# A deformable convolution and an embedding moved into the slots of an attention layer

## The chip, the cores and the metric

One core of a Trainium2 chip runs one program. It has five engines with a queue of instructions each: TensorE (PE), VectorE (DVE), ScalarE (ACT), GpSimd (POOL) and SyncE (SP), which issues most DMAs. An engine works through its queue in order and waits on semaphores for the others. The metric is device microseconds of one execution. The kernel before takes 12436.45 us, the median of 3 runs (12427.92 to 12447.01).

## The reference

Four layers follow each other on four images of 128 channels and 48x48 = 2304 positions: a selective scan (layer 0), a deformable convolution (layer 1), linear attention (layer 2), softmax attention (layer 3); after each of the last two comes a mixture of experts. What the change touches is layer 1 and the beginning of layer 2. Layer 1 samples the image at 9 taps per position, each at coordinates shifted by a small convolution's output, interpolates between four corners, and multiplies by a weight per tap:

```python
y0f = jnp.floor(py)
x0f = jnp.floor(px)
...
return v00 * (1 - wy) * (1 - wx) + v01 * (1 - wy) * wx + v10 * wy * (1 - wx) + v11 * wy * wx
...
sampled = _bilinear_gather(x, py, px) * mask[:, None]
out = jnp.einsum('oik,bikhw->bohw', weight.reshape(Co, C, 9), sampled)
...
return jax.nn.relu(out)
```

Layer 2 first normalises each position over its channels and embeds it, `h = x @ tok_W + tok_b + pe[None]`. Then follow eight blocks of attention over a whole image (each with its own weights), in which a position's keys are summed over the image before any query uses them, and a feed-forward part:

```python
t = t + attn(layer_norm(t, ln1_g[i], ln1_b[i]), i)
u = layer_norm(t, ln2_g[i], ln2_b[i])
t = t + (jax.nn.gelu(u @ W1[i] + b1[i], approximate=False) @ W2[i] + b2[i])
```

## The kernel before

Positions lie on the 128 partitions, channels in the free dimension. A tile is 128 positions (18 an image, `NT`), a block 3 tiles (384 positions; 6 an image, `NBLK`, 24 in all, `NBL`). The state `T`, called `h` in layer 2, holds all 72 tiles in SBUF.

Layer 0 writes each image to a table in DRAM, in which a row holds the four corners of one position (4 x 128 numbers), and the 27 offsets of each position to `offs`.

Layer 1 is `_layer1`. For each image, DVE makes from the offsets the table row of each tap (`idx`) and four corner weights with the mask in them (`wq`), in lines 949 to 982. Then tile after tile: POOL issues one gather of 128 table rows per tap into `g` (line 990; eight buffers), DVE multiplies the four corners by their weights into `gw` (line 997; four buffers), and PE multiplies each corner by the identity, which turns positions to the free dimension and adds the four up in PSUM (line 1003). ScalarE copies three taps at a time to `sT` (line 1006), PE multiplies nine taps by their weights (line 1009), adds the bias (line 1010), and ScalarE applies Relu (line 1011). The order of this part is left to a scheduler.

`_layer2` then embeds: for each image it measures means and deviations (`measure`, `finish`: batch statistics on DVE, a power on POOL), normalises (`normed`, line 1134), transposes (`transposed`, line 1146), multiplies by `tok_w` (line 1167) and adds `pe`, in which POOL has added the token's bias to the positions (line 1151). It keeps a copy of the layer's input in DRAM (`kept`) for the residual at the end.

The eight attention layers run as one chain of slots, whose order is written out by hand for PE, ACT, DVE and POOL. In slot s, counted through the layers at 24 blocks each, the key steps k1, k2, k3 work on block s; the query steps q0 to q2 on block s - 9 (`LAG`), q3 to q6 on block s - 10; the feed-forward f0 on block s - 11, f1 and f2 on s - 12 (`FLAG`), f3 and f4 on s - 13. So slots 0 to 8 hold key steps only, from 9 on queries join, from 12 on everything is there. After each image's sixth key block, `pieces` (the exponentials of the keys and the products `context`) are spread over the next slots. k0 normalises the next block on POOL and f0 on DVE; `biased` adds an output bias to a block of the state on POOL, right behind each of these two norms; `rotated` ends with an addition on POOL. The next layer's weights are created at slot 16 of a layer and prepared at slot 21.

A block of the code that sets the pace of layer 1:

```python
nc.gpsimd.indirect_dma_start(
...
gw = sp.tile([P, 4, C], F32, name="gw", bufs=4)
nc.vector.tensor_mul(
...
for q in range(4):
    nc.tensor.matmul(
        pt[:, t - t0, :], gw[:, q, :], ident, start=q == 0, stop=q == 3
    )
```

Of the kernel before, what the change touches and what calls it, by code (L numbers as in the profile page):

```python
# [15 lines left out]
F32 = mybir.dt.float32  # L16
# [894 lines left out]

def layer1(env, io, table, offs, T):


    with ExitStack() as ctx:
        _layer1(ctx, env, io, table, offs, T)


def _layer1(ctx, env, io, table, offs, T):
    nc, tc, ident = env.nc, env.tc, env.ident  # L920
    cp = ctx.enter_context(tc.tile_pool(name="l1c", bufs=1))
    sp = ctx.enter_context(tc.tile_pool(name="l1s", bufs=2))
    ps = ctx.enter_context(tc.tile_pool(name="l1p", bufs=3, space=PSUM))
    po = ctx.enter_context(tc.tile_pool(name="l1o", bufs=2, space=PSUM))
# [3 lines left out]
    w = cp.tile([P, TAPS, C], F32, name="w")  # L928
    nc.sync.dma_start(w, io["l1_w"])


    def row(name):
        t = cp.tile([P, C], F32, name=name)
        nc.scalar.dma_start(t, io[name].to_broadcast([P, C]))
        return t

    scale, shift, mean, var = (row("l1_" + n) for n in ("gamma", "beta", "mean", "var"))
    nc.vector.tensor_scalar_add(var, var, 1e-5)
    nc.scalar.sqrt(var, var)
    nc.vector.reciprocal(var, var)  # L940
    nc.vector.tensor_mul(scale, scale, var)
    nc.vector.tensor_mul(mean, mean, scale)
    nc.vector.tensor_sub(shift, shift, mean)
    for t in range(TAPS):
        nc.vector.tensor_mul(w[:, t, :], w[:, t, :], scale)

    for b in range(NB):
# [35 lines left out]
        for i in range(NT):  # L983
            sT = sp.tile([P, TAPS, P], F32, name="sT")
            for t0 in range(0, TAPS, 3):
                pt = ps.tile([P, 3, P], F32, name="pt")
                for t in range(t0, t0 + 3):
                    g = sp.tile([P, 4 * C], F32, name="g", bufs=8)
                    j = i * TAPS + t
                    nc.gpsimd.indirect_dma_start(  # L990
                        out=g,
                        out_offset=None,
                        in_=table,
                        in_offset=bass.IndirectOffsetOnAxis(ap=idx[:, j : j + 1], axis=0),
                    )
                    gw = sp.tile([P, 4, C], F32, name="gw", bufs=4)
                    nc.vector.tensor_mul(  # L997
                        gw,
                        g.rearrange("p (q c) -> p q c", c=C),
                        wq[:, i, t, :].unsqueeze(2).to_broadcast([P, 4, C]),  # L1000
                    )
                    for q in range(4):
                        nc.tensor.matmul(  # L1003
                            pt[:, t - t0, :], gw[:, q, :], ident, start=q == 0, stop=q == 3
                        )
                nc.scalar.copy(sT[:, t0 : t0 + 3, :], pt)
            out = po.tile([P, C], F32, name="out")
            for t in range(TAPS):
                nc.tensor.matmul(out, sT[:, t, :], w[:, t, :], start=t == 0, stop=False)
            nc.tensor.matmul(out, env.ones_row, shift[:1, :], start=False, stop=True)  # L1010
            nc.scalar.activation(T[:, b * NT + i, :], out, AF.Relu)
# [25 lines left out]
def layer2(env, io, T):  # L1037


    with ExitStack() as ctx:  # L1040
        _layer2(ctx, env, io, T)
# [5 lines left out]
FLAG = LAG + 3  # L1047

# [6 lines left out]
def _layer2(ctx, env, io, T):  # L1055
# [33 lines left out]
    tok_b = cp.tile([P, 1, C], F32, name="tok_b")  # L1089
# [25 lines left out]
    def measure(st, b, j):  # L1115
        mv, rstd = st
        s6 = sp.tile([P, G3, nc.vector.BN_STATS_DIM], F32, name="s6", bufs=3)
        for g in range(G3):
            nc.vector.bn_stats(out=s6[:, g, :], in_=h[:, b * NT + j * G3 + g, :])
            nc.vector.bn_aggr(out=mv[:, j * G3 + g, :], in_=s6[:, g, :])  # L1120
# [8 lines left out]
    def normed(st, b, j, engine, name):  # L1129
        mv, rstd = st  # L1130
        xn = sp.tile([P, G3, C], F32, name=name, bufs=1)
        for g in range(G3):
            i = j * G3 + g
            engine.tensor_scalar(  # L1134
                xn[:, g, :],
                h[:, b * NT + i, :],
                mv[:, i, 0:1],
                rstd[:, i : i + 1],
                op0=ALU.subtract,
                op1=ALU.mult,  # L1140
            )
        return xn
# [5 lines left out]

    pe = bp.tile([P, NT, C], F32, name="dk")
    nc.scalar.dma_start(pe, io["l2_pe"])  # L1150
    nc.gpsimd.tensor_add(pe, pe, tok_b.to_broadcast([P, NT, C]))
    st1 = []
    for b in range(NB):
        first = stats()
        for j in range(NBLK):
            nc.sync.dma_start(kept[:, at(b, j), :], h[:, at(b, j), :])
            measure(first, b, j)
        finish(first, 0, NT)
        st1.append(stats())
        for j in range(NBLK):  # L1160
            pt = psum(P, BLK)
            transposed(normed(first, b, j, nc.vector, "fn"), pt)
            xT = sp.tile([P, BLK], F32, name="uT", bufs=1)
            nc.scalar.copy(xT, pt)
            pp = psum(P, G3, C)
            for g in range(G3):
                nc.tensor.matmul(pp[:, g, :], xT[:, bass.ts(g, P)], tok_w, start=True, stop=True)
            nc.vector.tensor_add(h[:, at(b, j), :], pp, pe[:, j * G3 : (j + 1) * G3, :])
            measure(st1[b], b, j)
        finish(st1[b], 0, NT)  # L1170
# [32 lines left out]

    def biased(w, r, b, j):
        hb = h[:, at(b, j), :]
        nc.gpsimd.tensor_add(hb, hb, w["bias"][:, r : r + 1, :].to_broadcast([P, G3, C]))  # L1206

    def rotated(w, name, b0, b1, xT, j):
# [12 lines left out]
        nc.gpsimd.tensor_add(q, q, r)  # L1221
# [20 lines left out]
    def k0(y, n):  # L1242
        t, s, b, j = block(y, n)
        t["xn"] = normed(y.first[b], b, j, nc.gpsimd, "kn")
        biased(y.w, 0, b, j)

    def k1(y, n):
        t, s, b, j = block(y, n)
        col = y.w["col"]
        if j % (NBLK // 2) == 0:  # L1250
# [7 lines left out]
        t["xT"] = sp.tile([P, BLK], F32, name="xT", bufs=LAG + 2)  # L1258
# [45 lines left out]
    def largest_keys(s):  # L1304
# [7 lines left out]
        def tokens():  # L1312
# [4 lines left out]
            s["xb"] = sp.tile([P, P], F32, name="xb")  # L1317
# [225 lines left out]
    with tc.manual_schedule(engines=ORDERED):  # L1543
        for slot in range(-1, NL * NBL + FLAG + 3):
            i, n = divmod(slot, NBL)
            if i + 1 < NL and n == FLAG + 4:
                layers[i + 1] = Layer(i + 1, layers[i].after)
            if i + 1 < NL and n == NBL - 3:
                prepare(layers[i + 1].w)
            do(q0, slot - LAG)  # L1550
            do(f1, slot - FLAG)
            do(m0, slot - FLAG - 2)
            do(k1, slot)
            some(1)
            do(q3, slot - LAG - 1)
            do(f3, slot - FLAG - 1)
            do(k2, slot)
            do(f2, slot - FLAG)
            do(m1, slot - FLAG - 2)
            some(1)  # L1560
            do(q1, slot - LAG)
            do(k0, slot + 1)
            do(q4, slot - LAG - 1)
            some(1)
            do(k3, slot)
            do(whole, slot)
            do(f0, slot - FLAG + 1)
            do(q5, slot - LAG - 1)
            some(1)
            do(q2, slot - LAG)  # L1570
            some(1)
            do(m2, slot - FLAG - 2)
            do(q6, slot - LAG - 1)
            do(f4, slot - FLAG - 1)
            do(m3, slot - FLAG - 2)

# [662 lines left out]
def program(tc, io, out):  # L2239
    with ExitStack() as ctx:  # L2240
        env = Env(ctx, tc)
        nc = tc.nc
        with ExitStack() as conv:
            dr = conv.enter_context(tc.tile_pool(name="dr", bufs=1, space=DRAM))
# [147 lines left out]
```

## Time and profile before

| | us |
|---|---|
| median of 3 runs | 12436.45 |
| the profiled execution | 12545.34 |
| its span, first to last instruction | 12543.6 |
| layer 0, and layer 1's preparation | 0 to 5255.8 |
| gathers and products of layer 1 | 5255.8 to 6276 |
| embedding | 6276 to 6403 |
| layer 2's slots 0 to 20 | 6403 to 6733.8 |
| its slots 21 to 191 begin | 6733.8 to 10442.9 |
| rest (end of layer 2, experts, layer 3, experts) | to 12543.6 |

Times inside the span are counted from its first instruction. PE was granted 0.949 of its clock on the mean. Over the span PE is busy 87%, DVE 68%, ACT 55%, POOL 35%. A line of the profile names the line of the program, the engine, the operation, the tile written and, behind the arrow, the tiles read; for a group it then gives the number of instructions, the time in which at least one was running, the mean duration of one in ns, and the idle time of the engine just before them with what ended it. PE's products of full 32-bit numbers appear as two records each.

### The profile page before, as it was taken

To read this page: it belongs to the slowest core of one execution; us is meant where nothing else is said; L and a number is where in the kernel's file an instruction comes from. 1 tells how busy PE (TensorE), PEld (TensorE's weight loads), DVE (VectorE), ACT (ScalarE), POOL (GpSimd) and SP (SyncE) were. 2 spreads that over 40 slices of the span, in tenths; PEclk is the share of its full clock that TensorE was granted. 3 is DMA by queue.
4 is the path that set the end of the run, shared out by engine and by line. 5 is a ranking of instruction groups with operands and counts; after the bars stand their busy time and mean duration, and the time that the engine had idled before them with its cause. 6 is when DMAs were issued, how large, how long until landed. Compare 5 with 4: busy or idle time off the path is not lost.

```text
span 12543.6 us, 192625 instructions
## 1 busy us (share of the span) xinstructions
PE 10872.6 (87%) x71008; PEld 8365.3 (67%) x71008; DVE 8487.3 (68%) x15484; ACT 6888.6 (55%) x13190; POOL 4409.7 (35%) x4799
## 2 busy tenths in 40 slices
PE   7788787978887787688879999999999999698897
PEld 6667666766676666588857777777777777333333
DVE  6998989888988899544456656566566565455554
ACT  5777767777777777411135655555556555232332
POOL 2433434333333343366633333333333332100001
PEclk9999999999999999899979999999999999799998
DMA  3221222122212222356500000000000000300003
GB/s 122 68 70 63 80 77 71 63 76 80 70 64 76 79 67 67 111 171 177 170 21 2 4 3 3 4 2 4 2 3 5 1 1 12 115 7 8 8 8 126
DMA packets 329879, 677.51 MB, mean 54 GB/s; under 512 B 41556, under 2 KB 152168, under 8 KB 328048
## 3 DMA queue, kind: packets, MB, share of 16 engines
q1 hardware_dynamic: 276064, 493.50, 12.3%
q0 software_dynamic: 51840, 169.91, 4.8%
q8 instruction: 570, 9.34, 0.3%
q14 instruction: 365, 2.99, 0.1%
q10 hardware_dynamic: 1040, 1.77, 0.0%
HBM read 602.63 MB, written 71.85 MB: 54 GB/s over the span
## 4 chain that ended last, share of the span: by engine, by line
PE 43%; DVE 7%; ACT 3%; issue 1%; DMA 1%; POOL 1%; another core or an unknown queue 0%; SPq 0%; ACTq 0%; DVEq 0%; POOLq 0%
PE psum L1466 4%; PE pt L1003 4%; PE psum L1458 4%; PE pc L1352 3%; PE psum L1402 3%; PE scT L2105 3%; PE sc L2052 3%; PE out L2134 3%; PE psum L1372 2%; PE psum L1212 2%; PE psum L1213 2%; PE psum L1146 2%; PE psum L1290 1%; PE psum L1391 1%; DVE mx L1375 1%
## 5 line engine op out<-in xcount | busy, mean ns | idle before, releaser
L576 ACT ACTIVATE hs<-ps,bct 128x256 f32<-128x256 f32 x4608 | 1853.8, 474 | 1174.9 <-PE ps L570 1122.5
L570 PE MATMUL ps<-ident,h 128*128 128x128 f32 x9216 | 1491.9, 294 | 783.4 <-DVE h L556 612.7
L570 PEld LDWEIGHTS ps<-ident,h 128*128 128x128 f32 x9216 | 1079.7, 148 | 1168.7 <-DVE h L556 720.3
L584 PE MATMUL yp<-ident,hs 128*128 128x128 f32 x9216 | 1399.3, 288 | 28.5 <-ACT ys L599 28.5
L516 ACT ACTIVATE dA<-delta,l_Al 128x768 f32<-128x768 f32 x1536 | 1388.2, 936 | 0.3
L523 POOL TENSOR_TENSOR h<-du,rB 128x512 f32<-128x512 f32 x768 | 1077.5, 1403 | 757.9 <-PE ps L570 683.1
L584 PEld LDWEIGHTS yp<-ident,hs 128*128 128x128 f32 x9216 | 1151.2, 150 | 83.6 <-ACT ys L599 57.6
L556 DVE TENSOR_TENSOR_SCAN h<-dA,h 128x256 f32<-128x256 f32 (+1 forms) x1024 | 1084.4, 1059 | 27.3
L556 DVE TENSOR_TENSOR_SCAN h<-dA,carry,h 128x768 f32<-128x768 f32 x512 | 1027.1, 2006 | 10.5 <-ACT dA L516 10.5
L1206 POOL TENSOR_TENSOR T<-T,bias 128x384 f32<-128x384 f32 x384 | 383.7, 999 | 1563.5 <-DVE fn L1134 1523.2
L498 POOL TENSOR_SCALAR_AFFINE_SELECT dB<-bct 128x512 f32<-128x512 f32 x768 | 746.0, 971 | 358.4 <-PE b L530 240.9
L2113 ACT ACTIVATE pT<-scT 128x768 f32<-128x768 f32 (+2 forms) x504 | 377.6, 749 | 841.0 <-PE scT L2105 838.9
L530 PE MATMUL b<-dB,duT 128*128 128x128 f32 x6144 | 828.3, 279 | 0.8 <-ACT duT L456 0.8
L556 DVE TENSOR_TENSOR_SCAN h<-dA,carry,b 128x512 f32<-128x512 f32 x512 | 645.7, 1261 | 263.1 <-PE b L530 242.7
L1003 PE MATMUL pt<-ident,gw 128*128 128x128 f32 x5184 | 685.1, 294 | 147.2 <-DVE gw L997 117.6
L990 POOL DMA_INDIRECT g<-table,idx x648 | 659.9, 1018 | 390.0 <-DVE gw L997 189.6
L530 PEld LDWEIGHTS b<-dB,duT 128*128 128x128 f32 x6144 | 768.6, 196 | 2.4 <-POOL h L523 1.2
L1003 PEld LDWEIGHTS pt<-ident,gw 128*128 128x128 f32 x5184 | 650.1, 207 | 176.9 <-DVE gw L997 110.6
L997 DVE TENSOR_TENSOR gw<-g,wq 128x512 f32<-128x512 f32 x648 | 428.7, 692 | 496.9 <-PE pt L1003 416.7
L563 POOL COPY carry<-h 128x2 f32<-128x2 f32 x512 | 96.8, 189 | 1782.0 <-DVE h L556 1717.7
L2062 DVE TENSOR_REDUCE mx<-sc 128x2 f32<-128x1024 f32 (+3 forms) x400 | 428.3, 1071 | 345.2 <-PE sc L2052 340.2
L527 DVE TENSOR_TENSOR h<-du,rB 128x512 f32<-128x512 f32 x768 | 638.7, 832 | 1.6 <-DMA rB<-rows 1.4
(394 smaller groups left out, 22833.0 us busy)
## 6 DMA issues: line engine op xcount, KB each, us to landing
rB<-rows SPq DMA_DIRECT2D x768, 384.0 KB
w<-f_w SPq DMA_DIRECT2D x64, 1024.0 KB
table<-zero SPq DMA_DIRECT2D x162, 128.0 KB
table<-tok SPq DMA_DIRECT2D x16, 1152.0 KB
g<-table,idx POOLq DMA_INDIRECT x648
yd<-y SPq DMA_DIRECT2D x4, 2304.0 KB
sums<-raw SPq DMA_DIRECT2D x192, 48.0 KB
xb<-x SPq DMA_DIRECT2D x42, 192.0 KB
```

The source lines that it names most:

```text
L498: nc.gpsimd.affine_select(out=x.dB[n], in_=x.bc[:, m0 : m0 + CT // P, n : n + 1].to_broadcast([P, CT // P, P]), pattern=[[0, CT // P], [1, ...
L516: nc.scalar.activation(dA, x.delta[:, d, :], AF.Exp, scale=A[:, d, x.k, n : n + 1])
L523: nc.gpsimd.tensor_mul(h[:, 1, own], x.du[:, 1, own], x.rB[n][:, own])
L527: nc.vector.tensor_mul(x.h[n][:, :, own], x.du[:, :, own], b)
L530: nc.tensor.matmul(b0[:, bass.ts(m, P)], x.duT[:, m, :], x.dB[n][:, m, :], start=True, stop=True,)
L556: nc.vector.tensor_tensor_scan(h, da, b, initial=first, op0=ALU.mult, op1=ALU.add)
L570: nc.tensor.transpose(tt[:, m, bass.ts(d, P)], x.h[n][:, d, bass.ts(2 * q + m, P)], ident)
L576: nc.scalar.activation(hs, tt[:, m, :], AF.Copy, scale=x.bc[:, 2 * q + m, NS + n : NS + n + 1])
L584: nc.tensor.matmul(yp[:, q, (2 * d + m) * P : (2 * d + m + 1) * P], hs[:, bass.ts(d, P)], ident, is_transpose=True, start=n == 0 and m == ...
L990: nc.gpsimd.indirect_dma_start(out=g, out_offset=None, in_=table, in_offset=bass.IndirectOffsetOnAxis(ap=idx[:, j : j + 1], axis=0),)
L1003: nc.tensor.matmul(pt[:, t - t0, :], gw[:, q, :], ident, start=q == 0, stop=q == 3)
L1458: nc.tensor.matmul(pg, y.w["w1"][:, bass.ts(f, P)], t["uT"], start=True, stop=True)
```

## The change

`_layer1` is split. Its first half, now `positions_of`, computes rows and corner weights for all four images and writes them to DRAM (`index`, `corners`). The second half and the embedding move into `_layers12`, into the slots of layer 2: the chain of slots now begins at slot -3, and in slot s the convolution of block s + 3 (`AHEAD`) and the embedding of block s + 2 run between the steps of the attention. These become a list of small steps, dealt out over 17 places (`HOLES`) in the slot's order. The convolution takes place in slots -3 to 20, the embedding in -2 to 21.

Further:

- The corners of a tap are weighted in place, in their gather buffer. Of every third tap the four weighted corners are added to two on DVE. They are turned by accumulating transposes in place of products with the identity: 10 for three taps instead of 12.
- The weighing runs up to four taps (`WAHEAD`) ahead of the transposes. Weighings come in portions of one or two between the attention's steps.
- Gathers have six buffers of their own, and four more in the last image's place in the state as long as that is unused (16 blocks).
- While the convolution runs, the norm of k0 goes to ScalarE and the additions of `biased` and `rotated` to DVE (`spare`). The bias is then added in k1, a step behind the norm.
- Statistics of the embedding are taken block by block. `pe` with the token bias goes to DRAM (`pos`) and comes back a block at a time.
- The convolution's weights lie in the buffers of layer 2's weights of the second layer, so a layer is created at slot 22 and prepared at the same slot. `xT` has 9 buffers instead of 11, `xb` one instead of two.

The diff, cut to its core:

```diff
-        for i in range(NT):
-            sT = sp.tile([P, TAPS, P], F32, name="sT")
...
+        a = slice(b * NT, (b + 1) * NT)
+        nc.sync.dma_start(index[:, a, :], idx.rearrange("p (t k) -> p t k", k=TAPS))
+        nc.sync.dma_start(corners[:, a, :, :], wq)
...
+AHEAD = 3
+WAHEAD = 4
+HOLES = 17
+NG = 6
+NGT = 4
+NGTAPS = 16 * G3 * TAPS
...
+        if engine is nc.scalar:
+            own = slice(i0, i0 + G3)
+            shift = sp.tile([P, G3], F32, name="shift")
+            nc.vector.scalar_tensor_tensor(
+                shift, mv[:, own, 0], -1.0, rstd[:, own], op0=ALU.mult, op1=ALU.mult
+            )
+            for g in range(G3):
+                nc.scalar.activation(
...
+        def gather(self, k):
+            own = (self.n * G3 * TAPS + k) % (NG + NGT) - NG
+            if own >= 0 and self.n * G3 * TAPS + k < NGTAPS:
+                own = (NB - 1) * NT + own * 4
+                g = h[:, own : own + 4, :].rearrange("p q c -> p (q c)")
+            else:
+                g = sp.tile([P, 4 * C], F32, name="g", bufs=NG)
...
+        def weigh(self, k):
+
+            g = self.g[k].rearrange("p (q c) -> p q c", c=C)
+            nc.vector.tensor_mul(g, g, self.wq[:, k, :].unsqueeze(2).to_broadcast([P, 4, C]))
+            self.parts[k] = 4
+            if k % 3 == 0:
+                nc.vector.tensor_add(g[:, :2, :], g[:, :2, :], g[:, 2:, :])
+                self.parts[k] = 2
+
+        def turn(self, k0):
+
+            pt = psum(P, 3, P)
+            for k in range(k0, k0 + 3):
+                g = self.g.pop(k)
+                for q in range(self.parts[k]):
+                    nc.tensor.matmul(
+                        pt[:, k - k0, :],
+                        g[:, bass.ts(q, C)],
+                        ident,
+                        is_transpose=True,
+                        start=q == 0 and k == k0,
+                        stop=q + 1 == self.parts[k] and k == k0 + 2,
+                    )
...
+    def fetch(done):
+
+        nonlocal fetched
+        while fetched < min(done + NG + (NGT if done < NGTAPS else 0), NBL * G3 * TAPS):
...
+        def turn(k):
+            weigh(n * G3 * TAPS + k + 3)
+            sampled[n].turn(k)
+            fetch(n * G3 * TAPS + k + 3)
...
+    def spare():
+        return nc.vector if gathering else nc.gpsimd
+
     def biased(w, r, b, j):
         hb = h[:, at(b, j), :]
-        nc.gpsimd.tensor_add(hb, hb, w["bias"][:, r : r + 1, :].to_broadcast([P, G3, C]))
+        spare().tensor_add(hb, hb, w["bias"][:, r : r + 1, :].to_broadcast([P, G3, C]))
...
-        t["xn"] = normed(y.first[b], b, j, nc.gpsimd, "kn")
-        biased(y.w, 0, b, j)
+        engine = nc.scalar if gathering else nc.gpsimd
+        t["xn"] = normed(y.first[b], b, j, engine, "kn")
+        t["early"] = not gathering
+        if not gathering:
+            biased(y.w, 0, b, j)
...
-        for slot in range(-1, NL * NBL + FLAG + 3):
+        fetch(0)
+        for slot in range(-AHEAD, NL * NBL + FLAG + 3):
             i, n = divmod(slot, NBL)
-            if i + 1 < NL and n == FLAG + 4:
+            if 0 <= i < NL - 1 and n == max(FLAG + 4, NBL - AHEAD + 1):
                 layers[i + 1] = Layer(i + 1, layers[i].after)
-            if i + 1 < NL and n == NBL - 3:
+            if 0 <= i < NL - 1 and n == NBL - 2:
                 prepare(layers[i + 1].w)
+            early = convolve(slot + AHEAD)
+            steps = embed(slot + AHEAD - 1)
...
+            def one():
+
+                nonlocal passed
+                passed += 1
+                while early and (total - len(early)) * HOLES < total * passed:
+                    early.pop(0)()
+                if gathering:
+                    weigh((slot + AHEAD) * G3 * TAPS + G3 * TAPS * passed // HOLES + WAHEAD)
+
             do(q0, slot - LAG)
+            one()
             do(f1, slot - FLAG)
             do(m0, slot - FLAG - 2)
+            one()
             do(k1, slot)
             some(1)
+            one()
```

## The prediction

> **What bounds the kernel now.** I read the page's utilisation strips first, then the busy time by stretch, then the groups of the convolution's stretch, then single rows of its timeline.
>
> ```profile
> PE   7788787978887787688879999999999999698897
> DVE  6998989888988899544456656566566565455554
> POOL 2433434333333343366633333333333332100001
> ```
>
> A slice is 313.6 us. Layer 1 is slices 17 to 20 (5256 to 6276 us): TensorE (PE) is at 8, GpSimd (POOL) at 6, VectorE (DVE) at 4. From slice 21 on layer 2 holds PE at 9, DVE at 5 to 6, POOL at 3. Two stages with different idle engines stand one behind the other. By stretch:
>
> ```profile
> core 0: us, PE busy (x) PEld busy (x) DVE busy (x) ACT busy (x) POOL busy (x), PEclk, DMA share, GB/s
> 5260.00:5530.00 270.00, 224.18 (x1696) 212.38 (x1696) 130.67 (x247) 31.43 (x74) 181.23 (x173) 0.92 0.60 173
> 6276.00:6403.00 127.00, 60.53 (x220) 45.64 (x220) 71.35 (x353) 11.88 (x26) 28.45 (x13) 0.50 0.14 51
> 6403.00:6487.80 84.80, 71.96 (x352) 52.06 (x352) 33.45 (x83) 35.93 (x81) 42.68 (x47) 0.92 0.00 1
> 6487.80:6529.90 42.10, 39.82 (x226) 30.75 (x226) 30.42 (x86) 19.16 (x47) 19.25 (x22) 0.96 0.00 1
> 6529.90:6733.80 203.90, 197.27 (x1217) 157.78 (x1218) 117.32 (x367) 118.96 (x233) 72.64 (x84) 0.99 0.00 1
> ```
>
> Rows: a piece of the convolution; the embedding, in which nothing is full; layer 2's slots 0 to 8 (keys only), 9 to 11 (queries join), 12 to 20 (feed-forward joins). In the last, PE is busy 97%, 21.9 us of each slot's 22.7; DVE 13.0 us. A slot's start is its first scaled copy on ScalarE:
>
> ```profile
> 6402.99 0.67 ACT L1259 ACTIVATE xT<-psum,l_cols 128x384 f32<-128x384 f32 x1 [0.46 <-PE psum L1146]
> ...
> 6733.78 0.67 ACT L1259 ACTIVATE xT<-psum,l_cols 128x384 f32<-128x384 f32 x1
> ```
>
> These are slots 0 and 21. The change folds convolution and embedding into slots -3 to 20 and leaves the rest as it was, so I forecast when slot 21 starts.
>
> **The convolution's own prices.**
>
> ```profile
> L1003 PE MATMUL pt<-ident,gw 128*128 128x128 f32 x5184 | 685.1, 294 | 147.2 <-DVE gw L997 117.6 <-issue 29.1
> L990 POOL DMA_INDIRECT g<-table,idx x648 | 659.9, 1018 | 390.0 <-DVE gw L997 189.6 <-issue 153.5 <-ACT m L975 44.9
> L997 DVE TENSOR_TENSOR gw<-g,wq 128x512 f32<-128x512 f32 x648 | 428.7, 692 | 496.9 <-PE pt L1003 416.7 <-remote 52.7 <-issue 13.8
> L1009 PE MATMUL out<-w,sT 128*128 128x128 f32 x1296 | 165.6, 281 | 25.2 <-ACT sT L1006 19.0 <-issue 6.1
> ```
>
> A block is 3 tiles, 27 taps. L1003 has 5184 records for 2592 products: two passes each. In layer 2 the true transposes have one record each (L1391: 406 records in 45 slots of 9). A run of 72 passes of L1003 takes 8.30 us, 0.115 us a pass. Before, a block needs 216 passes for corners, 54 for weights and 6 for the bias: 31.7 us of PE work, and it takes 1007/24 = 42.0 us.
>
> **Part by part, for one slot (one block).**
>
> *PE.* Corners become accumulating transposes, and every third tap is first folded to two: 9 x 2 + 18 x 4 = 90. At one pass each 10.4 us, plus weights 6.2 and bias 0.7, plus the embedding (3 transposes at 0.135, the L1391 mean, and 6 passes) 1.1: 18.4 us. That such a transpose can accumulate at one pass is in no row; the ends are one pass (10.4) and two as in L1003 (20.7). I take one, since each transpose of layer 2 shows it.
>
> *DVE.* 27 weighings at 428.7/648 = 0.66: 17.9. Nine added foldings of 128x256 lie between 0.28 (128x128, L945) and 0.69 (128x512): 0.40 each, 3.6. The two statistics passes move in: 6 pairs at 0.272 + 0.182, 2.7. The sum with the positions 0.56; two bias additions and two rotary additions come over from POOL, about 0.55 each by the 128x384 additions, 2.2; four small ones at 0.17, 0.7. Together 27.6; with the slot's own 13.0, 40.6 us.
>
> *POOL.* Its next row is the crucial one: how long a gather's issue takes beside a busy DVE.
>
> ```profile
> 5530.16 2.68 DVE L997 TENSOR_TENSOR gw<-g,wq 128x512 f32<-128x512 f32 x4
> 5530.25 2.61 POOL L990 DMA_INDIRECT g<-table,idx  x1 [0.36 <-DVE fn L1134]
> ...
> 5806.70 4.42 DVE L997 TENSOR_TENSOR gw<-g,wq 128x512 f32<-128x512 f32 x7 [6.53 <-remote]
> 5807.66 1.15 POOL L990 DMA_INDIRECT g<-table,idx  x1 [2.53 <-DVE gw L997]
> 5809.11 0.95 POOL L990 DMA_INDIRECT g<-table,idx  x1 [0.30 <-issue]
> 5810.36 0.95 POOL L990 DMA_INDIRECT g<-table,idx  x1 [0.30 <-issue]
> ```
>
> Under seven weighings without a gap three gathers take 1.15, 0.95, 0.95, each 0.30 behind the last; one gather of 648, behind a normalising row, takes 2.61. I use the mean of 1.018 + 0.30 = 1.32: 35.6 us for 27, with 1.25 (0.95 + 0.30) and 2.91 as ends. Added are 2 to 4 powers for the deviations at 0.86. POOL: 36.5 us in slots -3 to -1, 37.3 in 0 to 8, 39.0 from 12 on. The norms and additions that POOL did in a slot (3 x 0.79 of L1134, 2 x 1.0 of L1206 and 2 x 1.0 of L1221, 6.4 us) go to ScalarE and DVE; kept there, they would make it the bound by far.
>
> [...]
>
> *ScalarE.* 9 copies at 0.48, 6 norms and 3 Relu at about 0.28, a copy 0.48: 7.3 on top of 118.96/9 = 13.2, half a slot. Hidden.
>
> *SyncE and DMA.* Per block index, corner weights, positions and a store, under 0.6 MB beside 7 MB of gathers; in layer 1 the DMA share was 0.60 at 42 us a block, so it has room. Layer 2's later weights wait for their old users only, so the later creation of a layer issues them no later; layer 1's reuse the convolution's weight buffers, released a slot before they are prepared.
>
> *Ahead of it.* Before, the first gather is at 5255.84. Now the index goes through DRAM, and POOL first adds the token bias to the positions (5.04 us before, at 6289.71), behind layer 2's constants on the queue. The four images' positions take about 4 us of DVE each from 5250, then the token bias's trip of about 2 us and the addition: 5273, first weighing 5276 (from a gather's start to its weighing the shortest in the trace is 3.46). Ends: 5262 and 5290. In return the constants' 12.6 us of waiting at 6276 go.
>
> **The sum.** Slots -3 to -1: 3 x 36 = 108. Slots 0 to 8: POOL 37.3 and two waits for a power behind the statistics, about 1 us each: 9 x 39.5 = 355. Slots 9 to 11: a third power, 3 x 41 = 123. From 12 on PE (21.9 + 18.4 = 40.3), DVE 40.6 and POOL 39.0 are all near 40, each queue in order, and the gather's spare buffers fall from ten to six at block 16 (slot 13). Friction: at worst what layer 1 shows, 42.0/31.7 = 1.32; at best layer 2's 22.7/21.9 = 1.03. I take 1.15: 46. Slots 14 and 20 carry an image's context and were 32.7 and 36.7; with 18.4, 51 and 55. So 43 + 6 x 46 + 51 + 55 = 425. Altogether 1011; slot 21 starts at 5276 + 1011 = 6287 instead of 6734: **447 us** less. Profiled run 12545.3 - 447 = 12098; the runs' median stands at 12436.45/12545.34 = 0.9913 of it: **11993 us**.
>
> **Rivals.**
> *The coupling costs as in layer 1.* For: three engines near 40, six buffers, weighing four taps ahead, so that DVE's queue can stand behind a gather in flight. Against: layer 1 had four buffers of weighed corners and no other work to fill in. 3 x 42 + 9 x 45 + 3 x 47 + 9 x 54 = 1158: 300 us gained, **12139**.
> *Everything overlaps at the rows' floor.* 3 x 34.6 + 9 x 35.5 + 3 x 36.3 + 7 x 40.6 + 51 + 55 = 922 from 5262: 550 gained, **11891**.
> *The transposes take two passes after all,* the change not doing what it says. PE from 12 on 50.6, POOL binding before: 108 + 355 + 3 x 43 + 9 x 53 = 1069: 389 gained, **12051**.
> *Gathers are held up by DVE,* 2.61 us each in every slot from 0 on: 27 x 2.91 + 3.4 = 82; 108 + 21 x 82 = 1830, slot 21 at 7106, 372 later: **12805, slower**. It turns from gain to loss at (6734 - 5276 - 108)/21 = 64.3 us a slot, a gather of 1.96 us. Against: only one gather of 648 was that long, and DVE's share there was 45%, where it would be about 90%.
>
> **Chances.** Forecast (11930 to 12070) 0.50; coupling 0.22; floor 0.15; two passes 0.05; between coupling and break-even 0.04; held-up gathers 0.04. Range 11870 to 12160, which takes in the ends of gathers at 1.25 and of friction at 1.32. What a measurement tells from no change is about 0.2%, 25 us. Faster 0.95, same 0.01, slower 0.04.
>
> **What would show it.** One record per corner transpose, 2160 in all (right), 4320 (two passes). Slots 0 to 8 at 37 to 42 us with POOL above 90% and gathers near 1.02 us; from 12 on 43 to 50 with PE, DVE and POOL all above 80%. First gather near 5273. A steady slot after 21 at 21.9 as before. It is wrong if gathers average over 1.3 us, if slots from 12 on exceed 55, or if later layers slow down.

## The result, and the profile after

The change makes the kernel 0.2% faster: 12430.03 us before (median of 12), 12406.06 us after (median of 12, 12398.04 to 12409.59), ratio 0.9978 with an interval of 0.9969 to 0.9987. 11993 us were forecast; the miss is 413 us, and the 24 us gained are a twentieth of the 447 that were forecast. One thing has to be known first: the kernel before runs in two conditions, near 12430 us and near 12530 us, on one chip at different times too (12434.82 and 12530.91 us); its profile shown above is of the second, the timed runs and the profile after are of the first (the first experiment shows where the difference lies).

The page of the kernel after, the strips that answer to those of before, with the granted clock:

```profile
PE   7778787977887787677779999999999998698897
DVE  6998989888988889666555565656566565445554
POOL 2443434333333334276443333333333332100001
PEclk9999999999999999888879999999999999799998
```

The mixed stage is slices 17 to 20 (the first is slice 0) and the beginning of 21. PE does not stay above 8 there, as was forecast for slots 12 on, but stands at 7; DVE has 5 to 6, POOL falls from 7 to 4, and the clock, 9 in most of layer 2 behind it, is 7 to 8. No engine is full. By stretch (slots -3 to -1, 0 to 8, 9 to 11, 12 to 20; columns as before):

```profile
5273.40:5407.00 133.60, 92.90 (x493) 74.58 (x493) 83.33 (x174) 20.71 (x51) 105.54 (x99) 0.73 0.70 200
5407.00:5795.70 388.70, 292.90 (x1785) 239.09 (x1783) 259.02 (x580) 104.44 (x252) 278.43 (x264) 0.89 0.62 177
5795.70:5961.60 165.90, 124.33 (x686) 102.95 (x685) 105.76 (x252) 44.46 (x103) 92.35 (x89) 0.81 0.47 136
5961.60:6602.80 641.20, 484.27 (x2686) 396.54 (x2684) 346.00 (x872) 194.88 (x403) 277.88 (x266) 0.82 0.36 102
```

| | forecast | after |
|---|---|---|
| first gather | 5273 | 5273.4 |
| slots -3 to -1 | 108 | 133.6 |
| slots 0 to 8 | 355 (39.5 each) | 388.7 (43.2) |
| slots 9 to 11 | 123 (41) | 165.9 (55.3) |
| slots 12 to 20 | 425 (47) | 641.2 (71.2) |
| slot 21 begins | 6287 | 6602.8 |

In the last stretch DVE's work is 346.0/9 = 38.4 us a slot (40.6 was forecast), POOL's 277.9/9 and 27 gaps of 0.30 make 39.0 (39.0 was forecast). The work of these two is what it was taken for. PE's is not: 484.3 us, where the forecast's 40.3 a slot make 363; the rest of the 641 us is waiting. What PE's corner transposes cost and waited for in slots 12 to 20:

```profile
L1210 PE MATMUL psum<-ident,g 128*128 128x128 f32 x764 | 169.5, 374 | 153.5 <-issue 103.2 <-DVE g L1198 37.6 <-DVE g L1201 4.7
```

PE's idle time of this stretch, 641.2 - 484.3 = 156.9 us, lies in front of this one line but for 3.4. A piece of slot 17 shows what it waits for:

```profile
6346.38 0.39 PE L1520 MATMUL psum<-l_sqsum,wqsq 128*128 128x8 f32 x2
...
6347.50 0.53 DVE L1524 TENSOR_REDUCE mx<-psum 128x8 f32<-128x352 f32 x1 [8.07 <-PE psum L1521]
...
6348.26 0.84 PE L1521 MATMUL psum<-proj,wq 128*128 128x352 f32 x2
...
6350.63 0.52 DVE L1527 TENSOR_TENSOR e<-psum,mx 128x352 f32<-128x352 f32 x1
6351.07 0.15 DVE L1097 SCALAR_TENSOR_TENSOR shift<-mv,rstd 128x3 f32<-128x3 f32 x1
6351.14 0.68 DVE L1198 TENSOR_TENSOR g<-g,wq 128x512 f32<-128x512 f32 x1
...
6352.38 2.52 PE L1210 MATMUL psum<-ident,g 128*128 128x128 f32 x10 [3.29 <-issue]
...
6355.82 1.25 PE L1210 MATMUL psum<-ident,g 128*128 128x128 f32 x10
```

DVE stands 8.07 us at `mx`, until PE has made the query's features; behind `mx` and `e` in its queue stands the weighing of three taps; PE's next instruction turns just these taps, and PE stands 3.29 us. They take turns. The ten transposes behind the pause take 2.52 us, the next ten 1.25.

### The profile page after: what moved, and what is told of

Same layout as the page of the kernel before. It is cut to its first block, busy times and chain, and to the rows that moved or that the text cites. A ratio compares the mean times of both kernels' runs of the same rounds, so it can differ in the third digit from the quotient of the medians.

```text
span 12404.9 us, 187225 instructions
## 1 busy us (share of the span) xinstructions
PE 10626.8 (86%) x67984; PEld 8068.9 (65%) x67984; DVE 8583.4 (69%) x15778; ACT 6951.9 (56%) x13328; POOL 4357.1 (35%) x4716
## 4 chain that ended last, share of the span: by engine, by line
PE 42%; DVE 9%; ACT 3%; DMA 2%; issue 2%; POOL 1%; SPq 0%; ACTq 0%; DVEq 0%; POOLq 0%
PE psum L1615 4%; PE psum L1607 4%; PE pc L1501 3%; PE psum L1551 3%; PE scT L2291 3%; PE sc L2238 3%; PE out L2320 3%; PE psum L1521 2%; PE psum L1356 2%; PE psum L1210 2%; PE psum L1357 2%; PE psum L1123 2%; PE psum L1439 2%; PE psum L1227 1%; PE psum L1540 1%
## 5 line engine op out<-in xcount | busy, mean ns | idle before, releaser
L1350 POOL TENSOR_TENSOR T<-T,bias 128x384 f32<-128x384 f32 x353 | 353.2, 1001 | 1454.8 <-DVE fn L1111 1438.8
L1188 POOL DMA_INDIRECT g<-table,idx x476 | 499.9, 1050 | 392.4 <-PE psum L1210 174.4
L1441 DVE TENSOR_REDUCE kmax<-psum 128x8 f32<-128x352 f32 x576 | 275.3, 519 | 435.8 <-ACT dk L1440 429.3
L1210 PE MATMUL psum<-ident,g 128*128 128x128 f32 x1588 | 329.9, 355 | 272.8 <-issue 149.7
L1615 PE MATMUL psum<-w,gl 128*128 128x128 f32 x4608 | 547.5, 275 | 1.9 <-ACT wqsq L1363 1.5
```

The costliest lines, as they stand in the source:

```text
L1188: nc.gpsimd.indirect_dma_start(out=g, out_offset=None, in_=table, in_offset=bass.IndirectOffsetOnAxis(ap=self.idx[:, k : k + 1], axis=0),)
L1210: nc.tensor.matmul(pt[:, k - k0, :], g[:, bass.ts(q, C)], ident, is_transpose=True, start=q == 0 and k == k0, stop=q + 1 == self.parts[k] ...
L1615: nc.tensor.matmul(pp[:, g, :], t["gl"][:, f, bass.ts(g, P)], y.w["w2"][:, f, :], start=f == 0, stop=f == DFF // P - 1,)
```

## The experiments

The table has every run of the kernel after and its variants, in us per slot. "Late" is the sum, from the first gather to slot 24, of the waits whose releaser the trace calls "remote": it found none that had ended just before. Late starts is the name here for the condition in which there are such waits. e10_six_and_lead has few of them and yet belongs to it, as the last section shows; e3_no_gathers, with its ten gathers, has none. Single runs have no ratio. The times of e2, e3 and e9 are of kernels that compute something else, as told below.

| run | late | slots 0-8 | 9-11 | 12-20 | ratio to before, interval |
|---|---|---|---|---|---|
| after (again: e5_after_again) | 0 (0) | 43.2 (43.1) | 55.3 (55.3) | 71.2 (71.2) | 0.9978, 0.9969 to 0.9987 (0.9983, 0.9974 to 0.9993) |
| e14_after_same_chip | 112 | 50.7 | 56.8 | 71.1 | 0.9969, 0.9958 to 0.9981 |
| e2_no_weighing | 268 | 44.3 | 47.2 | 55.2 | |
| e3_no_gathers | 0 | 41.6 | 55.2 | 67.8 | |
| e4_ahead_15 | 185 | 50.1 | 14.2 | 22.2 | 0.9933, 0.9916 to 0.9949 |
| e6_weigh_10_ahead | 0 | 41.3 | 42.8 | 58.3 | 0.9834, 0.9818 to 0.9851 |
| e13_lead_same_chip | 128 | 45.7 | 48.2 | 58.9 | 0.9812, 0.9797 to 0.9827 |
| e11_weigh_7_ahead | 89 | 46.2 | 51.2 | 60.4 | |
| e7_warm_16 | 0 | 46.9 | 56.7 | 67.7 | |
| e8_six_buffers | 0 | 49.2 | 57.1 | 70.7 | |
| e10_six_and_lead | 5 (has late starts) | 47.6 | 51.4 | 60.7 | |
| e9_more_buffers | 104 | 45.5 | 47.2 | 54.3 | 0.9785, 0.9772 to 0.9799 |
| e12_handover | 148 | 45.6 | 48.3 | 53.0 | 0.9778, 0.9764 to 0.9791 |
| e17_weigh_14 | 0 | 47.8 | 52.4 | 57.8 | 0.9924, 0.9907 to 0.9940 |

### Which profile of before belongs to the times

The kernel before, unchanged, three times more.

> The kernel before, unchanged, profiled once more. Its first profiled execution took 12545 us, its other runs 12423 to 12447. If that execution was an odd one: about 12430 us, and the stage whose span shrinks by some 100 us (I look at the convolution first, 5256 to 6276) is where my sum started from too long a time. If the profiler always slows this kernel: again about 12540 us.

> The kernel before once more, for its stages on the chip of the other three: from the first gather to slot 0 1147 to 1152 us, as on the first two profiles, if the chip is of the slower kind or if the chips differ elsewhere; 1040 to 1060 if it is of the faster kind and the difference lies in the convolution and the embedding.

> The kernel before once more. Its three profiles so far (spans 12537 to 12547 us) all show engines of the convolution started up to 12 us late with the releaser 'remote', 118 to 164 us of such waits in all, and no such wait outside it; the kernel after has none of them where the kernel before beside it took 12435 us, and has 109 us of them where it took 12531. If those waits are the 100 us between the two conditions, a profile of the kernel before with a time near 12435 shows no 'remote' wait and 1040 to 1070 us from the first gather to slot 0; if the time is near 12535, this stays open.

12548.84, 12538.93 and 12427.92 us. The third had no late starts. Its gathers and weighings, from the page:

```profile
L990 POOL DMA_INDIRECT g<-table,idx x648 | 709.1, 1094 | 242.3 <-issue 152.5 <-ACT m L975 45.0 <-DMA g<-table,idx 23.4
L997 DVE TENSOR_TENSOR gw<-g,wq 128x512 f32<-128x512 f32 x645 | 444.6, 694 | 423.6 <-DMA g<-table,idx 358.8 <-PE pt L1003 53.6 <-PE out L1010 7.8
```

Compare with the rows that the prediction quotes: there L997 waits 416.7 us for PE and 52.7 for "remote", here 358.8 for gathers, 53.6 for PE and nothing remote. The stage from the first gather to slot 0 is 1045.1 us, against 1147.2 in the profile before. A block takes 908.5/24 = 37.9 us and POOL issues without a gap worth naming: 27 x (1.094 + 0.30) = 37.6. So 102 of the 117 us between the two executions' spans (12543.6 and 12426.2) lie in the convolution and the embedding alone, and in the condition of the timed runs POOL's issue of gathers, not PE, already set the pace there. From this profile's slot 21 (6630.3) to that of after (6602.8) are 27.5 us, near the 24.0 between the medians.

### Is it the weighing or the gathers?

Theory A: PE waits for weighings that stand in DVE's queue behind attention rows which wait for PE. Theory B: gathers and buffers set the pace. First without the weighing (the corners go unweighted and unfolded into the same transposes), then with ten gathers only (every later tap weighs and turns what lies in its buffer):

```diff
-            nc.vector.tensor_mul(g, g, self.wq[:, k, :].unsqueeze(2).to_broadcast([P, 4, C]))
```

> The changed kernel with the corners' weighing and folding left out (the products with the corner weights are missing; numbers of transposes, gathers and copies stay). Theory A (in slots 9 to 20 TensorE's next transposes stand behind a weighing, and that weighing stands in VectorE's queue behind attention rows which themselves wait for TensorE, so that the two take turns): slots 12 to 20 fall from 71 us to 42 to 50, the granted clock there from 0.82 to above 0.95, the run to about 12100 us. Theory B (gathers, POOL's queue and the six buffers set the pace): slots 12 to 20 stay above 60, the run above 12300 us.

> The changed kernel with the first ten gathers only; later taps weigh and transpose whatever stands in the same rotating buffers, so the buffers' order of use stays and POOL's work and the DMA go (the sampled data are wrong). Theory A: slots 12 to 20 stay at 62 to 71 us, the run at 12300 to 12400 us (the slots without queries, which POOL binds, fall from 43 to about 33 us). Theory B: slots 12 to 20 fall below 50 us, the run below 12150 us.

Without weighing, slots 12 to 20 take 55.2 us in place of 71.1, and 9 to 11 take 47.2 in place of 56.8 (beside e14, which has late starts too); without gathers 67.8 in place of 71.2, and nothing changes in 9 to 11. From slot 9 on the weighing costs far more than the gathers. It came short of A's 42 to 50 us and of its clock (0.91, above 0.95 was expected), with more late starts than any other run; 12254 us lie between both theories' times. In slots 0 to 8 neither decides alone: 41.6 without gathers, where A expected 33.

### The convolution earlier

```diff
-AHEAD = 3
+AHEAD = 15
```

> The changed kernel with the convolution 15 blocks ahead in place of 3 (one number): it runs alone in slots -15 to -1, beside the key steps in slots 0 to 8, and not beside queries and feed-forward. Theory A: alone about 38 us a slot, with keys 42, slots 9 to 20 as in the kernel before (246 us for all twelve): 5276 + 15 x 38 + 9 x 42 + 246 = 6470, so slot 21 starts 130 us earlier than in the changed kernel, about 12275 us. Theory B (gathers set the pace at 44 us everywhere): 5276 + 24 x 44 + 246 = 6578, about 12380 us.

Slots -15 to -1 take 44.2 us each, as B had them: POOL issues 27 gathers in 37 us, each 0.30 us behind the last, and then waits 3 us for the statistics. The key slots take 50.1, over both theories, and as long as in the kernel after with late starts (50.7, e14); slots 12 to 20 take 22.2, as before the change. Slot 21 begins at 6651 and the kernel takes 12442.8 us, later than both theories had it; they reckoned without late starts. Ratio 0.9933, beside 0.9969 for the change with late starts, on another chip. Putting the convolution where the attention is thin is worth some 45 us; it doesn't say why the dense slots are slow.

### How far ahead is four taps ahead?

The code says it, and I had not counted it. A slot has 16 small steps for 17 places, so one each: transposes of three taps at places 1 to 3, 5 to 7, 10, 12 and 13. The weighing is dealt out evenly, to 27 p / 17 + 4 taps by the end of place p. When place 6 comes, 12 are weighed and its transposes need 15; at place 13, 24 of 27. `turn` then weighs what lacks, right there. So in eight of nine groups the last tap is weighed in the same place as its transposes (the expectation below says seven; this is the recount), in five all three. The lead is used up by place 6.

```diff
-WAHEAD = 4
+WAHEAD = 10
```

> The kernel after, unchanged, on the chip of the next three, so that stages are compared on one chip. If the difference of chips lies in the stages the change doesn't touch, the stages between the first gather and slot 21 repeat within 1%: slots 0 to 8 at 41 to 44 us, 9 to 11 at 55, 12 to 20 at 70 to 72, and the first gather to slot 21 at 1315 to 1345. If it lies in the convolution or the slots, they differ by some 100 us in all.

> WAHEAD 10 in place of 4; nothing else. Theory A: the portions of weighing are dealt out evenly (27 taps over 17 places), but the nine groups of transposes stand in places 1 to 3, 5 to 7, 10, 12 and 13, so with four taps of lead seven of the nine groups have their last tap weighed in the same place, right in front of them: TensorE waits while VectorE first finishes rows that wait for TensorE. With ten taps every group's last tap is weighed one to five places earlier; then slots 9 to 11 fall from 55 to 44 to 49 us and slots 12 to 20 from 71 to 46 to 58 (55 is what they took without any weighing), the time by 110 to 230 us. Theory B: the gathers' landing sets the pace and six buffers allow no lead; weighing earlier makes VectorE stand behind gathers in flight, so slots 0 to 8 rise above 45 us and slots 12 to 20 stay above 68.

> WAHEAD 7: by the dealing, three of nine groups still have their last tap weighed in the same place as their transposes, against seven with four and none with ten. If the lead of the last tap is the cause, slots 9 to 12 lie between 43 (ten) and 57 (four), at 44 to 50, and slots 13 to 20 at 59 to 66. If ten taps helped for another reason (a fuller VectorE queue, say), there is no reason for a value between.

12228.8 us with ten, ratio 0.9834 beside 0.9983 for the kernel after on the same chip; e5_after_again repeats the stages to 0.1 us a slot. Slots 0 to 8, 9 to 11 and 12 to 20 with ten taps:

```profile
5402.90:5774.30 371.40, 289.94 (x1795) 235.35 (x1796) 266.20 (x589) 103.49 (x254) 286.20 (x267) 0.88 0.65 186
5774.30:5902.80 128.50, 104.94 (x681) 87.41 (x681) 106.88 (x252) 41.18 (x103) 97.19 (x88) 0.93 0.62 175
5902.80:6427.60 524.80, 414.88 (x2680) 347.49 (x2680) 348.77 (x868) 186.03 (x403) 277.50 (x268) 0.88 0.45 126
```

Slots 9 to 11 take 42.8 us (41 was forecast), slot 12 alone 42.9, slots 12 to 20 58.3, with the same work for DVE and POOL; theory A's ranges are missed by little, below and above, and theory B's by far. The same line of PE in slots 12 to 20:

```profile
L1210 PE MATMUL psum<-ident,g 128*128 128x128 f32 x760 | 116.2, 295 | 108.2 <-DVE g L1201 54.9 <-DVE g L1198 50.0 <-DVE rstd L1087 2.1
```

Its waiting fell from 153.5 to 108.2, its work from 169.5 to 116.2. Over all its lines PE waits 47 us less in these slots (156.9 to 109.9) and works 69 us less (484.3 to 414.9) with the same instructions: more than half of the gain is PE running faster (mean clock 0.88 in place of 0.82). Seven taps lie between four and ten (51.2 between 56.8 and 48.2, 60.4 between 71.1 and 58.9, all three with late starts): theory A, in the form of the missing lead, holds.

### The clock

```diff
+            for _ in range(WARM):
+                nc.tensor.transpose(pt[:, 0, :], ident, ident)
```

> Sixteen transposes of the identity are put ahead of each group of transposes, into the same PSUM place, which the first true transpose overwrites: added work of 16 x 0.115 = 1.8 us a group, 16.6 a slot, that waits for no weighing. Theory C: the pauses cost above all because the granted clock falls to a half behind them (ten transposes took 2.52 us behind a pause, 1.25 otherwise); the filler keeps the clock up, the mean granted clock in slots 12 to 20 rises from 0.82 above 0.93, and the slots take 60 to 68 us in place of 71 in spite of the added work. Theory A: the pauses are waits for VectorE whatever the clock; the filler lies in them or adds to them, and slots 12 to 20 take 71 to 82 us.

Slots 12 to 20 with the filler:

```profile
6002.50:6612.00 609.50, 546.70 (x3949) 474.32 (x3947) 346.20 (x872) 193.53 (x404) 281.78 (x266) 0.97 0.38 108
```

The clock is 0.97 in place of 0.82, and the slots take 67.7 us although the filler adds 17.6 us of work to each (158.7 us in the trace). That is what theory C expected, and not what A did. PE's other work falls from 484 us to about 390 (546.7 less the filler), over 10 us a slot; the filler itself eats most of that. So the halved clock is a large part of what the pauses cost, and not an alternative to the missing lead: behind the pauses in the rows below it is 0.50, and with lead its mean rises from 0.82 to 0.88. As a remedy the filler is worth nothing: in slots 0 to 8, with less waiting to fill, it costs 3.8 us, and the whole kernel takes 12417.98 us beside 12416.59.

The trace of the kernel after has the granted clock beside PE's work. The clock changes in it at steps of 3.41 us; around the piece shown above:

| window | PE's work in it, us | clock in it |
|---|---|---|
| 6335.17 to 6338.59 | 1.01 | 1.00 |
| 6338.59 to 6342.00 | 3.27 | 0.50 |
| 6348.83 to 6352.24 | 0.27 | 1.00 |
| 6352.24 to 6355.65 | 3.27 | 0.50 |
| 6355.65 to 6359.06 | 3.41 | 1.00 |

In these rows a window has half the clock behind one in which PE worked 1.01 us or less, and the full one behind one in which it worked 3.27. PE was not idle throughout the windows ahead of the halved ones: the pauses there are of 2.41 us (to 6338.26) and 3.29 us (to 6352.38). From 6352.24 to 6355.65 PE ran nothing but transposes (15, of L1210 and L1123), and the clock behind them was full.

### Buffers

Six buffers throughout, with four taps of lead and with ten:

```diff
-NGT = 4
+NGT = 0
```

> Six gather buffers throughout, none in the last image's place. Theory A: the lead of the weighing is at most four taps in any case, so slots 0 to 8 stay within 3 us of 43 and slots 9 to 12 within 3 us of the kernel after's. Theory B: buffers set the pace, and the step from ten to six explains the rise at slot 13; slots 0 to 8 rise to 48 to 52 us (50 is what they took with AHEAD 15, where these slots had six), slots 9 to 12 by 7 us or more each.

> WAHEAD 10 and six buffers throughout. If lead and buffers are needed together, six buffers cancel most of the lead in slots 9 to 12: 50 to 60 us in place of 43, and slots 0 to 8 stay at 47 to 51 as with six buffers and four taps of lead; slots 13 to 20 stay at 58 to 62. If lead alone counts, slots 9 to 12 stay at 41 to 47.

Without lead, six buffers change nothing from slot 12 on (70.7) and cost 6.1 us in slots 0 to 8 (49.2): theory B was right for slots 0 to 8 and A from slot 9 on. With lead they cost 3.2 us in slots 9 to 11 (51.4 beside 48.2 of e13; both runs have late starts), of the 8.6 that lead gains there. Lead needs buffers: a tap weighed early stays in its buffer longer, and the code weighs no tap before its gather is issued, which with six buffers is at most six taps ahead of the transposes. With ten taps of lead the waits of slots 12 to 20, of which 13 to 20 have six buffers, are headed by

```profile
DVE g L1198 <- DMA g<-table,idx: 123.6, 119, 4.5
```

and in the kernel after it was

```profile
POOL g L1188 <- PE psum L1210: 150.9, 44, 11.2
PEld psum L1210 <- issue: 127.3, 36, 4.2
```

So the last image's buffers were kept longer, given up one by one as the convolution's blocks need their place:

```diff
-NGTAPS = 16 * G3 * TAPS
+LASTS = (18, 19, 20, 22)
...
+            while free[0] is not None and LASTS[free[0]] < self.n:
+                free.pop(0)
+            own = free.pop(0)
+            free.append(own)
...
+            if fetched >= done + NG + sum(x >= fetched // (G3 * TAPS) for x in LASTS):
+                break
```

> WAHEAD 10, and the four gather buffers in the last image's place are given up one by one, each when the block that writes there comes: ten up to block 18, then nine, eight, seven, seven, and six for block 23. With ten taps of lead and buffers to six at slot 13, slots 9 to 12 took 43 us and slots 13 to 20 took 60, with VectorE waiting 121 us there for gathers to land. If the six buffers are what keeps slots 13 to 20 from the 43 us of slot 12, slots 13 to 15 (blocks 16 to 18) fall to 43 to 50, slot 14 with its context to 55, and slots 16 to 20 lie between that and 60, highest at the end: 50 to 90 us less than with ten taps alone, 12140 to 12180 beside a kernel before of 12435. If PE and VectorE together, each in order, hold them at 60, nothing changes: 12215 to 12240.

> As the run with more buffers, with the hand-over mended: a gather is issued only when the buffer it takes has been turned (there, at each of the four steps from ten to six, one gather came a step too early and overwrote a tap). Ten buffers through block 18, then nine, eight, seven, seven, six. If buffers are what remains beside the lead, its ratio to the kernel before lies 0.4 to 0.7% under that of ten taps of lead alone: 0.976 to 0.980 beside 0.983, and slots 13 to 15 take 48 to 58 us in place of 60. If the early gather was what shortened that run, it equals ten taps alone.

> The kernel with ten taps of lead once more, beside the other three on one chip. The ratio repeats at 0.982 to 0.985 if the gain is not a matter of the chip.

> The kernel after once more. Two chips so far ran the kernel before in 12530 us and two in 12435. If the difference lies in how fast gathers land, then on a chip of the first kind the slots 0 to 8 of this kernel take 45 us or more in place of 43, and on one of the second kind the convolution of the kernel before takes less than 1020 us. If it lies elsewhere, these stages repeat.

The first of them counted the buffers by the block being turned, so that at each of the four steps one gather overwrote a tap not yet turned; e12 counts them by the block being fetched, and takes about as long. The first ran over the time it was expected to take, and over its slots 14 and 15 (49.9, 58.4 and 56.2 from slot 13 on); that expectation reckoned without late starts. 12251.6 us beside 12530.91: ratio 0.9778, against 0.9812 with lead alone and 0.9969 after, all on one chip and with late starts. Slots 13 to 15 take 50.5, 57.2 and 49.0 us, against 56.8, 65.8 and 58.9, as e12 was expected to; its distance to lead alone is 0.34%, a little under the 0.4 expected. This is the fastest version that computes the same: 2.2% under the one before. e13 repeats the gain of lead alone with late starts, its ratio a little under the range expected. e14's 50.7 us in slots 0 to 8 fit its expectation, but that gathers landing slower is the reason isn't shown. What PE waits for in its slots 12 to 20 (the line numbers moved by three):

```profile
L1213 PE MATMUL psum<-ident,g 128*128 128x128 f32 x576 | 84.3, 286 | 46.8 <-DVE g L1201 25.1 <-issue 12.8 <-DVE g L1204 3.4
...
L1213 PE MATMUL psum<-ident,T 128*128 128x128 f32 x210 | 31.6, 286 | 10.0 <-DVE T L1201 7.8 <-issue 2.1
```

56.8 us in place of 153.5, and the clock there is 0.93. At 53.0 us a slot these slots still stand over the 47 of the forecast; the runs don't separate what is left, late starts among it. More lead on the same buffers:

> WAHEAD 14 with the mended hand-over. If the last tap's lead of one to three places still leaves TensorE waiting (86 us before the transposes in 500 us with ten taps and more buffers), a lead of three places and more takes part of that away: slots 12 to 20 at 49 to 52 us in place of 53, ratio 0.974 to 0.977. If VectorE then stands behind gathers in flight, slots 0 to 8 and 12 to 20 rise by 1 to 3 us and the ratio to 0.979 to 0.983.

Worse than either branch expected: 0.9924, slots 0 to 8 at 47.8, and without late starts at that. In these slots DVE waits for gathers

```profile
DVE g L1201 <- DMA g<-table,idx: 81.5, 90, 4.7
...
DVE T L1201 <- DMA T<-table,idx: 56.0, 60, 4.7
```

137.5 us, against 43.3 + 31.3 = 74.6 with ten taps. Here DVE does stand behind gathers in flight: with ten buffers no gather is issued more than ten taps ahead, so fourteen asks for taps whose gathers have just been issued. Of the leads tried (4, 7, 10, 14) ten is the best: far enough for a tap to be weighed a place before its transposes, not so far that the gather has not landed.

## Why the prediction was wrong

- **The friction of 1.15 for slots 9 to 20 failed.** It was put between 1.03 and 1.32, from stages in which one queue leads, and a reason was missing for either. Measured: 71.2/40.6 = 1.75, because the order written out gives the weighing no lead: DVE waits for PE at the attention's rows, PE waits for the weighings behind them. The text's own sign of being wrong, slots from 12 on over 55 us, came. It argued with "weighing four taps ahead" without counting at which place each weighing and each group of transposes is issued. Of the 318 us by which the four terms of slots were short, 216 are in slots 12 to 20 and 43 in 9 to 11. Ten taps of lead alone take 154 us of them back (58.3 against 71.2 nine times, 42.8 against 55.3 three times).
- **Six buffers from slot 13** were named, and not priced. In the kernel as it is they are no part of the miss (70.7 us a slot with six throughout, 71.2 without). With lead they cost (58.9 - 53.0) x 9 = 53 us.
- **The clock was taken as full.** Granted were 0.81 and 0.82 from slot 9 on. Of the 216 us in slots 12 to 20, about 120 are PE's work taking longer than the sum had it (484 in place of 363), the rest is more waiting. The clock rose where the waits fell: 0.93 in place of 0.81 in slots 9 to 11 with ten taps.
- **Slots -3 to 8 were 59 us short** (25.6 and 33.7). In slots 0 to 8 ten taps of lead leave 41.3 us, and there POOL's queue is full: gathers at 1.074 + 0.30, 27 of them 37.1 us, and powers with their waits. Issue beside DVE is a little dearer than the 1.018 taken. Of slots -3 to -1 the filling was left out: block 0's last Relu comes 45.7 us after the first gather, the next two 37.6 and 40.3 later.
- **The scaling failed too.** The forecast difference was taken from a profile with late starts and the whole scaled by 0.9913. 12098 for the profiled run missed by 309; the other 105 are the scaling, which spread over the whole kernel what lay in the very stage that the change removes, so that the late starts of the profile were taken off twice. The row of L997 had "remote 52.7" in it, and the median stood 109 us lower: both were quoted and not put together.
- **"What bounds the kernel now" fell with it:** 42.0 us a block over 31.7 of PE's work was taken as the price of coupling (1.32); without late starts it is 37.9, POOL's issue.
- **Right:** the first gather (5273.4, right behind POOL's addition of 5.03 us, as the text had it), the work of DVE and POOL by slot, one record per transpose (1588 + 572 = 2160), gathers not held up (1054 ns on the mean, with DVE busy 54 to 67%), slot 24 on at 21.9 us.
- **The rivals:** "the coupling costs as in layer 1" had the mechanism (DVE's queue behind something in flight) but the wrong partner, and its 54 us a slot was 17 too few. No rival was "the order written out gives no lead".

Not settled: what brings the late starts. Slots -15 to -1 of e4_ahead_15 at a constant 44.2 us seem to belong to them: from 5400 to 5900 us ScalarE's Relu `T` (L1231) stands idle 79.4 us in ten waits called "remote", 9.9 us in the longest.

## What to carry to other kernels

Where steps are dealt out over places by hand, write down for each pair of producer and consumer at which place each is issued: a lead given as a constant is gone when consumers come in bunches and producers evenly. Three engines at 40 us of work each in one slot give the slot's floor and not its length; the order in their queues decides that, here between 53 and 71 us, and lead and buffers have to be bought together. When the profiled execution differs from the median, find the stage the difference lies in before scaling.

## What the runs showed of the hardware

The kernels with gathers ran in two conditions. With late starts, an engine stands idle for some time although what it waits for is done, only while gathers run: 131 to 164 us of such waits in the kernel before at 12537 to 12547 us of span, none at 12426. In the profile before ScalarE's copy `sT` at 5395.61 begins 5.57 us after the products that it copies have ended, at 5390.04; the longest such wait of `sT` in e15_before_same_chip is 12.3 us, the longest of all 16.2 us (e2). One and the same chip showed both conditions at different times (the kernel before in 12434.82 us beside e5 to e8, in 12530.91 us beside e12 to e15), so it is not the chip alone. Slots 0 to 8 of the kernel after, with late starts (the two largest waits of that kind):

```profile
ACT hT L1221 <- remote: 22.1, 5, 5.3
ACT v L1435 <- remote: 14.3, 4, 6.5
```

e3_no_gathers has none. Where there are late starts, the traces counted (before, e14, e10) have fewer updates of the semaphores than instructions that make one. In the profile before, from the first gather to slot 0, there are 780 updates of PE's semaphore for 818 instructions; all but one of the engines of the waits called "remote" begin within 0.03 us of an update, `sT` at 5395.61 of one at 5395.59, late as it is. From the first gather to slot 21 the trace of e14 has 1067 updates for 1174 instructions, that of the kernel after 1174 for 1174. By this count e10 (1063 for 1195) has late starts too. What makes the updates fewer and late is open.

In absolute time the kernel before loses 101 us to late starts (12531 beside 12430), the change 83 and the version with lead 64. That the kernels with the convolution hidden lose less is not clear of noise: the ratios with and without late starts (0.9969 and 0.9978 for the change, 0.9812 and 0.9834 with lead) have intervals that overlap.
